# Layer 3's transposed transition matrix: VectorE block transposes into a packed tile in place of TensorE transposes

## The chip, the core and the metric

The kernel runs on one core of a Trainium2 chip. The metric is the device time in microseconds (us) of one execution, the median of several. A core has five engines that run side by side and wait for one another through semaphores: TensorE (matmuls, results in PSUM), VectorE, ScalarE and GpSimd (elementwise work), and SyncE, which here issues the DMAs. In the profile they are PE (with PEld for the loading of weights), DVE, ACT, POOL and SP.

## The reference, cut to what matters

Four graph layers run over 128 graphs of 64 nodes with 512 features. Each layer adds its result to x after a layer norm and a ReLU of its input. Layer 3, the one that is changed, makes a 64x64 transition matrix T for each graph and spreads the features with T and with T squared:

```python
h = jnp.maximum(_layernorm(x, axis=-1), 0.0)
...
Xw = X @ Wv + bv                       # X is h
sj, si = Xw @ aw[:d, 0], Xw @ aw[d:, 0]
e = jax.nn.leaky_relu(sj[:, None, :] + si[:, :, None] + ab[0], negative_slope=0.2)
alpha_matrix = A * jnp.exp(e)
transition = alpha_matrix / (jnp.sum(alpha_matrix, axis=-1, keepdims=True) + 1e-12)
for k in range(Wk.shape[0]):           # 3 steps
    H = H + Xk @ Wk[k] + bk[k]
    Xk = jnp.einsum('bij,bjd->bid', transition, Xk)
return jax.nn.relu(H)
```

So layer 3 is h·W0 + T·h·W1 + T·T·h·W2 plus biases. The adjacency is (128, 64, 64), all numbers are 32-bit floats.

## The kernel before, in words

**Tiling.** A tile is 128 rows of x, that is two graphs; a group is four tiles (T = 4), eight graphs, and there are 16 groups. Each 64x64 matrix of a pair of graphs stands in a 128x128 block-diagonal tile `bd`, [128, 4, 128] for a group. `HALVES` are the two halves of the 128 partitions. Phase 1 runs layers 0 and 1 over all groups and writes the half-finished x to DRAM; phase 2 loads it again and runs layers 2 and 3. The large weight products use a Strassen scheme with seven products (`seven`, `strassen`): every `L595` in the profile is one of its matmuls in layers 0, 1 and 3, and every `L818` one in layer 2.

**What sets the order.** Nothing is issued in the order of the text. Each layer function only records operations (`pe`, `dve`, `act`, `pool`, `dma`) with an estimated cost, the buffers they read and write, and a priority. `Graph.run` then plans: it goes through time, on each engine takes from the operations that can start earliest the one with the smallest priority, gives buffers their slots, and writes the instructions out in that order. The hardware engines execute their queues strictly in that order. A priority is a due time: a base per group (`PERIOD1` or `PERIOD2` times the group's number), plus the progress inside a layer (`step`, scaled by `STRETCH`), plus the offset of the named part in `AT`. All these constants are tuning knobs: they change no result, only the order of the instructions. The planner also overlaps neighbouring groups, so layer 2 of one group stands between the products of layer 3 of the group before.

**Around the change.** In `layer3`, `z` becomes the 64x64 weights of the attention; L904 to L906 sum and invert them by row, and the two L908 write the normalised T into the block-diagonal `tr`. Then TensorE transposes the four 128x128 blocks against the identity (L915) into a PSUM bank, ScalarE copies that bank into plane 0 of the tile `tt` (L917), TensorE multiplies T with it for the transposed square (L921), and ScalarE copies that into plane 1 (L923). The left products `lm` (L936) then multiply h, for each half of the partitions, with both planes: 64 rows of h against `tt.t[half, t, :, half]`, which is 2 x 64 columns, and two copies (L940) bring the result into the layer's Strassen operand `a3`. Only the diagonal 64x64 blocks of `tt` are used there; the tile holds 128 columns per plane, half of them zero. The additions L587 form the Strassen combinations; L565, L567, L953 and L954 take the products out of PSUM, with GpSimd's L949 in between.

Four other lines are named later. L651, L655, L901 and L902 make z, and L651 first waits for a row that two DMAs (L633, L637) have sent through DRAM. L844 are layer 2's 64-column attention scores, L834 and L830 make their query operand, and L879 are layer 2's products with the values, which wait for L854 (the attention weights) and L869 (the values).

**Memory.** PSUM has eight banks (`ps`), shared by all. The list `TWO` places buffers of phase 2 over those of phase 1; `tt` had one slot of [128, 4, 2, 128].

Of the kernel before, what the change touches and what calls it, by code (L numbers as in the profile page):

```python
# [14 lines left out]
P = 128  # L15
C = 64
D = 512
DH = 1024
T = 4
KD = D // P  # L20
KH = DH // P
EPS = 1e-5
HALVES = (slice(0, C), slice(C, P))
# [138 lines left out]
def tile_adj_preln_d4(  # L162
# [6 lines left out]
    nc = tc.nc  # L169
# [18 lines left out]
        ([("tmp", [P, D], 4), ("mB", [P, T, C + 1], 1)], [("s3", [P, 3, 6, P], 1)]),  # L188
        ([("z", [P, DH], 2)], [("hT", [P, KD, T * P], 1)]),
        ([("rT", [P, KH, P], 3)], [("a3", [P, 3 * KD, P], 2)]),  # L190
        ([("s2", [P, 3, 4, P], 1), ("s1", [P, 3, 2, P], 2)], [("vu", [P, 2, D + 1], 2), ("tt", [P, T, 2, P], 1)]),
        ([("y", [P, D], 2)], [("qT", [P, 2, 2 * P], 2)]),
        ([("mT", [P, KD, P], 3)], [("a3", [P, 3 * KD, P], 1)]),
        ([("row", [P, D], 5)], [("sh", [P, 4, 2, 2 * P], 1), ("q", [P, D], 1)]),
# [5 lines left out]
    def size(shape):  # L200
        n = 1
        for d in shape[1:]:
            n *= d
        return n

    for two in TWO:
        both = work.tile([P, max(sum(size(shape) * n for _, shape, n in tags) for tags in two)], F32,
                         name="_".join(tag for tags in two for tag, _, _ in tags))
        for tags in two:
            at = 0  # L210
            for tag, shape, n in tags:
                for i in range(n):
                    v = both[:, at:at + size(shape)]
                    at += size(shape)
                    if len(shape) == 3:
                        v = v.rearrange("p (a b) -> p a b", a=shape[1])
                    elif len(shape) == 4:
                        v = v.rearrange("p (a b c) -> p a b c", a=shape[1], b=shape[2])
# [25 lines left out]
    def c_mm(n, count):  # L244
        return 2 * count * max(n * 2 / 2400 + 0.0025, 0.111)

    TR = 0.109
# [4 lines left out]
    def pe(cost, fn, r, w):  # L252
        return G.op("PE", cost, fn, r, w)

    def dve(cost, fn, r, w):
        return G.op("DVE", cost, fn, r, w)

    def act(cost, fn, r, w):
        return G.op("ACT", cost, fn, r, w)
# [7 lines left out]
    def quad(b):  # L267
        return b.t.rearrange("p (c k) -> p c k", c=4)

    STRETCH, PERIOD1, PERIOD2 = (2.01, 1.52, 3.8, 3.15), 99.32, 100.99
    AT = {
        "x0": -1000.31, "apart": -0.04, "w1": -1140.59, "b1": -730.1, "w2": -692.69, "w": 166.49, "c1": -856.63,
        "l0": -580.98, "c2": -741.75, "l1": 111.32, "c": 219.34, "g0": -1134.91, "g1": -1116.26, "g2": -755.63,
        "g3": -850.44, "g": -1126.24, "l3": 28.03, "wg": 119.55, "w3": 191.39, "last": -98.19, "load1": -120.84,
        "load2": -92.69, "m": -52.0, "h0": -37.33, "p0": -2.35, "z0": -2.26, "q0": 25.57, "y0": -29.58, "h1": -39.25,
        "p1": -17.85, "z1": 10.94, "q1": 12.3, "y1": 27.38, "s": -11.54, "t0": 62.66, "e0": -103.04, "t1": 54.99,
        "e1": -32.68, "hT": -26.23, "sh": 50.82, "lq": 16.73, "pt": 40.17, "v": -3.1, "pv": -184.92, "s3": 16.54,
        "tt": 62.29, "a0": 61.26, "b0": -39.87, "a1": 81.07, "b1_": 65.71,  # L280
    }

    def part(name):
        G.shift = AT[name]


    ident = const.tile([P, P], F32, name="ident")
# [82 lines left out]
    def dot(in0, in1, acc, r, w):  # L370
        j = Buf("o")
        dve(0.77, lambda: nc.vector.scalar_tensor_tensor(j.t, in0(), 1.0, in1(), op0=ALU.mult, op1=ALU.mult,
                                                         accum_out=acc()), r, [*w, j])
# [140 lines left out]
    def pre_stats(g, t):  # L514

        xx, nm = xt[g, t], Buf("nm")
        mv, rs = norm_stats(lambda i: xx.t, 1, [xx])
        pool(0.3, lambda: nc.gpsimd.tensor_scalar(nm.t, mv.t[:, 0:1], rs.t, -1.0, op0=ALU.mult, op1=ALU.mult), [mv, rs], [nm])  # L518
        return nm, rs

    def pre_ln(g, t, stats=None):

        xx, h = xt[g, t], Buf("h")
        nm, rs = stats or pre_stats(g, t)
        act(0.82, lambda: nc.scalar.activation(h.t, xx.t, AF.Relu, bias=nm.t, scale=rs.t), [xx, nm, rs], [h])  # L525
        return h
# [362 lines left out]
    def layer3(g):  # L889

        ad = adjs[g]
        a3, ss = [Buf("a3") for _ in range(T)], [Buf("col"), Buf("col")]
        part("s3")
        stats = [pre_stats(g, t) for t in range(T)]
        for t in range(T):
            h = pre_ln(g, t, stats[t])
            for s in range(2):
                dot(lambda h=h: h.t, lambda s=s: c3_b[:, s, :], lambda t=t, s=s: ss[s].t[:, t:t + 1], [h, ("c3", s)], [(ss[s], t)])
        z = bcast_sum(lambda: ss[1].t, lambda: ss[0].t, [(ss[s], t) for t in range(T) for s in range(2)], extra=kap)
        lrelu(z, 0.2)  # L900
        act(0.42, lambda: nc.scalar.activation(z.t, z.t, AF.Exp), [z], [z])  # L901
        dve(0.42, lambda: nc.vector.tensor_mul(z.t, z.t, ad.t[:, 0]), [z, ad], [z])  # L902
        dn, rn, tr, tt = Buf("col"), Buf("col"), Buf("bd"), Buf("tt")
        dve(0.42, lambda: nc.vector.tensor_reduce(dn.t, z.t, AX.X, ALU.add), [z], [dn])  # L904
        dve(0.16, lambda: nc.vector.tensor_scalar_add(dn.t, dn.t, 1e-12), [dn], [dn])
        dve(0.18, lambda: nc.vector.reciprocal(rn.t, dn.t), [dn], [rn])  # L906
        for s in HALVES:
            dve(0.42, lambda s=s: nc.vector.tensor_mul(tr.t[s, :, s], z.t[s], rn.t[s, :, None].to_broadcast([C, T, C])), [z, rn], [(tr, s.start)])  # L908
        trk, pt, p2 = [(tr, 0), (tr, C)], Buf("ps"), Buf("ps")

        part("tt")

        def mt():
            for t in range(T):
                nc.tensor.transpose(quad(pt)[:, t, :], tr.t[:, t, :], ident)  # L915
        pe(KD * TR, mt, trk, [pt])
        act(0.59, lambda: nc.scalar.copy(tt.t[:, :, 0, :], quad(pt)), [pt], [(tt, 0)])  # L917

        def m2():
            for t in range(T):  # L920
                nc.tensor.matmul(quad(p2)[:, t, :], tr.t[:, t, :], tt.t[:, t, 0, :], start=True, stop=True)  # L921
        pe(c_mm(128, T), m2, [*trk, (tt, 0)], [p2])
        act(0.59, lambda: nc.scalar.copy(tt.t[:, :, 1, :], quad(p2)), [p2], [(tt, 1)])  # L923
        step(2.0)
        for t0 in (0, 2):
            part("a0" if t0 == 0 else "a1")
            for t in (t0, t0 + 1):
                h, b, back = pre_ln(g, t, stats[t]), a3[t], Buf("q")
                transposed(lambda h=h: h.t, [h], Buf("o"), lambda back=back: back.t, [back], lambda b=b: b.t[:, :KD, :], [(b, 0)])

                pq = [Buf("ps"), Buf("ps")]

                def lm(h=h, pq=pq, t=t):
                    for c in range(KD):
                        for i, half in enumerate(HALVES):
                            nc.tensor.matmul(quad(pq[i])[:, c, :], h.t[half, c * P:(c + 1) * P], tt.t[half, t, :, half],  # L936
                                             start=True, stop=True)
                pe(c_mm(128, KD) + 0.2, lm, [h, (tt, 0), (tt, 1)], pq)
                for i, half in enumerate(HALVES):
                    act(0.59, lambda pq=pq, b=b, i=i, half=half: nc.scalar.copy(  # L940
                        b.t[:, KD:, half].rearrange("p (j c) k -> p c j k", j=2),
                        pq[i].t.rearrange("p (c j k) -> p c j k", c=KD, j=2)), [pq[i]], [(b, 1 + i)])
                step(1.0)

            def emit_o(i, j, p, u, v, t0=t0):
                xx, cols, (U, iv) = xt[g, t0 + i], slice(j * D // 2, (j + 1) * D // 2), v
                add, ka = (lambda: bk3_b[:, cols]), "bk3"
                if u is not None:
                    pool(0.88, lambda: nc.gpsimd.tensor_add(U.t[:, iv], U.t[:, u[1]], add()), [u, ka], [v])  # L949
                    add2, ka = (lambda: U.t[:, iv]), v  # L950
                else:
                    add2 = add
                dve(c_v(D // 2), lambda: nc.vector.tensor_add(U.t[:, iv], p.t[:, :D // 2], add2()), [p, ka], [v])  # L953
                dve(c_v(D // 2), lambda: nc.vector.scalar_tensor_tensor(xx.t[:, cols], U.t[:, iv], 0.0, xx.t[:, cols], op0=ALU.max, op1=ALU.add), [v, xx], [(xx, j)])  # L954
                if (i, j) in ((1, 0), (0, 1)):
                    r = (g * T + t0 + i) * P
                    dma(256, lambda: nc.sync.dma_start(out[r:r + P, :], xx.t), [(xx, 0), (xx, 1)], [])

            ak = {}
            for i in range(2):  # L960
                b = a3[t0 + i]
                ak[i, 0] = [(b, 0), (b, 1), (b, 2)]
                ak[i, 1] = [(b, 1), (b, 2)]
            part("b0" if t0 == 0 else "b1_")
            strassen(lambda i, j, t0=t0: a3[t0 + i].t[:, 6 * j:6 * j + 6, :], ak, W3, 6, D // 2, "s3", emit_o)

    def step(us):

        G.prio += us * stretch[0]
# [32 lines left out]
    for k in range(3):  # L1002
        src = Wk3[k].rearrange("(c p) o -> p c o", p=P)
        for c in (0, 2):
            i = k * KD + c
# [69 lines left out]
```

## Time and profile before

| What | Value |
|---|---|
| median of 3 runs | 2401.43 us (2398.42 to 2402.01) |
| profiled execution | 2396.96 us, span 2395.1 us, TensorE clock 0.998 |
| span of phase 1 and phase 2 | about 0 to 1190 and 1190 to 2395 us |
| one group of phase 2 in the steady part | 73.2 us (L915 at 1540.97, the same step of others a multiple of 73.2 later) |
| L915, 64 records | mean 275 ns, 9.8 us busy in all |
| L921, 128 records | mean 276 ns, 17.0 us busy in all |
| L936, 1024 records | mean 278 ns, 65.8 us busy in all |
| L917 and L923, 16 each | 585 ns each |
| L908, 32 | 420 ns each |

A 32-bit matmul shows as two records, a transpose as one. Records of matmuls overlap, because they are pipelined: a mean of 275 ns does not mean that the engine was held for 275 ns, and what a piece of work costs is read from where the next one starts. An entry of the timeline gives start, length, engine, line, tiles, shape and count; brackets at its end hold the idle time just before it and what ended it.

### The profile page before, as it was taken

The page shows a single profiled execution, that of the slowest core. Times are in us where ns is not written, and L with a number is a line of the kernel's source. Part 1 is how long each engine was busy: PE and PEld are TensorE (multiplying, and loading weights), DVE is VectorE, ACT ScalarE, POOL GpSimd, SP SyncE. Part 2 cuts the span into 40 slices and gives each one's busy share as a digit, 9 for nine tenths or more (in the row PEclk, how much of TensorE's full clock was granted, in tenths as well). Part 3 has the DMA queues.
Part 4 walks back from the last instruction along what each step waited for, and adds up shares of the span by engine and source line. Part 5 has one row for each costly group of instructions (what it writes and reads, how often), then busy time and mean ns, then how long its engine had stood idle before and what let it go on. Part 6 is the DMA issues. An engine that isn't in the chain of part 4 may idle for free.

```text
span 2395.1 us, 33543 instructions
## 1 busy us (share of the span) xinstructions
PE 2356.3 (98%) x11930; PEld 1855.0 (77%) x11930; DVE 1721.2 (72%) x3676; ACT 1263.5 (53%) x1754; POOL 938.2 (39%) x1450
## 2 busy tenths in 40 slices
PE   7999999999999999999999999999999999999999
PEld 3576677776777776777778888888888888888887
DVE  7887878787878787877878556666666666666664
ACT  2666565566565566565745445544445444454431
POOL 5234455434455434455344333333333333333321
PEclk9999999999999999999999999999999999999999
DMA  7232222232223222222532232222322222222211
GB/s 242 54 80 47 65 68 71 68 78 51 65 66 73 67 80 52 61 67 77 146 89 62 66 74 55 69 56 58 78 64 60 66 50 71 73 56 64 52 42 36
DMA packets 335928, 168.78 MB, mean 70 GB/s; under 512 B 284688, under 2 KB 290832, under 8 KB 335760
## 3 DMA queue, kind: packets, MB, share of 16 engines
q1 hardware_dynamic: 335760, 166.63, 28.0%
q8 instruction: 94, 1.54, 0.3%
q14 instruction: 74, 0.61, 0.1%
HBM read 64.76 MB, written 34.70 MB: 42 GB/s over the span
## 4 chain that ended last, share of the span: by engine, by line
PE 84%; DVE 6%; DMA 4%; ACT 2%; POOL 2%; issue 2%; SPq 0%; DVEq 0%; POOLq 0%; ACTq 0%
PE ps L595 60%; PE ps L818 11%; PE ps L534 4%; PE ps L936 2%; PE ps L731 2%; PE ps L879 2%; DVE s_s_vu_tt L869 1%; DMA x<-xm 1%; PE ps L844 1%; ACT o L543 1%; DVE bd L854 1%; ACT h L525 1%; POOL u L867 1%; POOL rs L511 1%; DVE st L508 1%
## 5 line engine op out<-in xcount | busy, mean ns | idle before, releaser
L525 ACT ACTIVATE h<-x,nm,rs 128x512 f32<-128x512 f32 x384 | 307.1, 813 | 456.5 <-POOL nm L518 455.3
L595 PE MATMUL ps<-wb_mem,rT_a 128*128 128x256 f32 x2056 | 476.8, 380 | 1.7 <-DVE z_hT L615 0.9
L595 PEld LDWEIGHTS ps<-wb_mem,rT_a 128*128 128x128 f32 x2056 | 386.5, 190 | 74.8 <-issue 20.3
L510 POOL TENSOR_SCALAR rs<-mv 128x1 f32<-128x1 f32 x320 | 101.5, 317 | 534.2 <-DVE mv L509 452.9
L595 PE MATMUL ps<-wb_mem,s_s_vu_tt 128*128 128x256 f32 x1152 | 275.0, 379 | 0.2 <-DVE s_s_vu_tt L587 0.2
L595 PE MATMUL ps<-wb_mem,tmp_mB_s 128*128 128x256 f32 x1152 | 261.3, 379 | 0.2 <-DVE tmp_mB_s L587 0.2
L595 PEld LDWEIGHTS ps<-wb_mem,s_s_vu_tt 128*128 128x128 f32 x1152 | 218.5, 190 | 43.1 <-issue 10.5
L595 PE MATMUL ps<-wb_mem,mT_a 128*128 128x256 f32 x1016 | 240.7, 380 | 1.8 <-ACT u L563 1.3
L595 PEld LDWEIGHTS ps<-wb_mem,tmp_mB_s 128*128 128x128 f32 x1152 | 217.6, 190 | 29.6 <-DVE tmp_mB_s L587 0.6
L595 PE MATMUL ps<-wa_mem,mT_a 128*128 128x512 f32 x512 | 238.0, 593 | 2.1 <-DVE u L567 2.1
L949 POOL TENSOR_TENSOR u<-u,bk_b 128x256 f32<-128x256 f32 x96 | 76.2, 799 | 352.3 <-DVE u L567 292.6
L511 POOL TENSOR_TENSOR rs<-rs,mhalf 128x1 f32<-128x1 f32 x320 | 202.9, 634 | 26.6
L595 PEld LDWEIGHTS ps<-wb_mem,mT_a 128*128 128x128 f32 x1016 | 190.6, 190 | 28.6 <-ACT u L563 1.5
L508 DVE BATCH_NORM_STATS2 st<-x 128x6 f32<-128x512 f32 x256 | 174.1, 680 | 32.4 <-DMA x<-xm 30.8
L595 PE MATMUL ps<-wa_mem,s_s_vu_tt 128*128 128x512 f32 x384 | 182.9, 599 | 1.0 <-ACT c_b L453 0.6
L595 PEld LDWEIGHTS ps<-wa_mem,mT_a 128*128 128x128 f32 x512 | 96.0, 190 | 105.4 <-issue 92.5
L565 DVE TENSOR_TENSOR u<-ps,u 128x256 f32<-128x256 f32 (+1 forms) x160 | 84.4, 527 | 112.1 <-PE ps L595 84.6
L623 POOL TENSOR_TENSOR u<-u,row_sh_q 128x256 f32<-128x256 f32 x96 | 70.9, 746 | 235.0 <-DVE u L565 205.9
L545 ACT COPY rT_a<-z_hT 128x1024 uint16<-128x1024 uint16 x128 | 144.3, 1161 | 4.4 <-DMA z_hT<-tmp_mB_s 4.2
L534 PEld LDWEIGHTS ps<-bd,h 128*128 128x128 f32 x1024 | 129.0, 192 | 16.1 <-issue 8.6
L707 ACT ACTIVATE z_hT<-z_hT 128x512 f32<-128x512 f32 x128 | 79.8, 625 | 116.7 <-DVE z_hT L615 116.6
L563 ACT COPY u<-ps 128x256 f32<-128x256 f32 (+1 forms) x160 | 72.5, 453 | 129.7 <-PE ps L818 71.5
(172 smaller groups left out, 4317.1 us busy)
## 6 DMA issues: line engine op xcount, KB each, us to landing
x<-in_x_dram SPq DMA_DIRECT2D x64, 256.0 KB, 2.8
xm<-x SPq DMA_DIRECT2D x64, 256.0 KB, 2.0
x<-xm SPq DMA_DIRECT2D x64, 256.0 KB, 2.7
out_dram<-x SPq DMA_DIRECT2D x64, 256.0 KB, 2.2
adj<-in_adj_dram SPq DMA_DIRECT2D x32, 256.0 KB, 4.1
rw<-row SPq DMA_DIRECT2D x96, 64.0 KB, 2.8
wb_mem<-in_Wk_dram SPq DMA_DIRECT2D x6, 512.0 KB, 4.4
wa_mem<-in_W1T_dram SPq DMA_DIRECT2D x2, 1024.0 KB, 5.9
```

The lines of the kernel that those rows point to most:

```text
L508: dve(0.69, lambda i=i: nc.vector.bn_stats(st.t[:, i, :], src(i)), [r[i]], [(st, i)])
L510: pool(0.3, lambda: nc.gpsimd.tensor_scalar_add(rs.t, mv.t[:, 1:2], EPS), [mv], [rs])
L511: pool(0.65, lambda: nc.gpsimd.tensor_tensor(rs.t, rs.t, mhalf, ALU.pow), [rs], [rs])
L525: act(0.82, lambda: nc.scalar.activation(h.t, xx.t, AF.Relu, bias=nm.t, scale=rs.t), [xx, nm, rs], [h])
L534: nc.tensor.matmul(quad(p)[:, c, :], h.t[:, c * P:(c + 1) * P], rhs(), start=True, stop=True)
L545: act(1.16, lambda: nc.scalar.copy(u16(dst()).rearrange("p c (k q) -> p c k q", q=2), u16(back()).rearrange("p (q c r) -> p c r q", q=2, c ...
L563: act(n / 1200 + 0.17, lambda: nc.scalar.copy(at(0)(), p1.t[:, :n]), [p1], [(U, 0)])
L565: dve(c_v(n), lambda: nc.vector.tensor_add(at(1)(), p2.t[:, :n], at(0)()), [p2, (U, 0)], [(U, 1)])
L595: nc.tensor.matmul(p.t[:, :n], lhs()[:, c, :], rhs(c), start=first and c == 0, stop=c == kc - 1, skip_group_check=True)
L707: act(0.63, lambda: nc.scalar.activation(z.t[:, cols], z.t[:, cols], AF.Relu), [(z, j)], [(z, j)])
L818: nc.tensor.matmul(pair(p.t)[:, o, :], a, b, start=first and o == 0 and c == 0, stop=c == 1, skip_group_check=True)
L949: pool(0.88, lambda: nc.gpsimd.tensor_add(U.t[:, iv], U.t[:, u[1]], add()), [u, ka], [v])
```

## The change

VectorE can transpose 32x32 blocks from SBUF to SBUF. A 64x64 block is four such blocks, swapped across the diagonal. The change makes the transposed T that way, directly behind L908: for each half of the partitions four instructions, each of which takes a 32 x (4 tiles x 32) block of `tr` to its mirrored place in `tt`. It is for taking the four transposes off TensorE, and with them one PSUM bank, one ScalarE copy and one hand-over between engines. Since the two diagonal blocks of a tile stand on different partitions, `tt` need only hold 64 columns a plane: it is packed to [128, 4, 2, 64], and gets two slots in the memory of the one before. The square then has 64 moving columns for 128, and its copy half the elements. The left products read the same numbers, now from adjacent columns. And the constants of the planner (`STRETCH`, the periods, `AT`) are tuned anew, which reorders the work of all engines in both phases.

```diff
-        ([...], [("vu", [P, 2, D + 1], 2), ("tt", [P, T, 2, P], 1)]),
+        ([...], [("vu", [P, 2, D + 1], 2), ("tt", [P, T, 2, C], 2)]),
...
-    STRETCH, PERIOD1, PERIOD2 = (2.01, 1.52, 3.8, 3.15), 99.32, 100.99
+    STRETCH, PERIOD1, PERIOD2 = (2.01, 0.85, 5.07, 2.81), 97.12, 109.98
     AT = {
-        ... "s3": 16.54, "tt": 62.29, "a0": 61.26, "b0": -39.87, "a1": 81.07, "b1_": 65.71,
+        ... "s3": -5.11, "tt": -20.18, "a0": 57.03, "b0": -53.42, "a1": 66.82, "b1_": 64.98,
...
-        trk, pt, p2 = [(tr, 0), (tr, C)], Buf("ps"), Buf("ps")
+        trk, p2 = [(tr, 0), (tr, C)], Buf("ps")
+
+        B = C // 2
+
+        def blocks(s):
+            for i in range(2):
+                for j in range(2):
+                    nc.vector.transpose(tt.t[s.start + j * B:s.start + (j + 1) * B, :, 0, i * B:(i + 1) * B],
+                                        tr.t[s.start + i * B:s.start + (i + 1) * B, :, s.start + j * B:s.start + (j + 1) * B])
+        for i, s in enumerate(HALVES):
+            dve(1.2, lambda s=s: blocks(s), [(tr, s.start)], [(tt, 2 + i)])

         part("tt")
-
-        def mt():
-            for t in range(T):
-                nc.tensor.transpose(quad(pt)[:, t, :], tr.t[:, t, :], ident)
-        pe(KD * TR, mt, trk, [pt])
-        act(0.59, lambda: nc.scalar.copy(tt.t[:, :, 0, :], quad(pt)), [pt], [(tt, 0)])

         def m2():
             for t in range(T):
-                nc.tensor.matmul(quad(p2)[:, t, :], tr.t[:, t, :], tt.t[:, t, 0, :], start=True, stop=True)
-        pe(c_mm(128, T), m2, [*trk, (tt, 0)], [p2])
-        act(0.59, lambda: nc.scalar.copy(tt.t[:, :, 1, :], quad(p2)), [p2], [(tt, 1)])
+                nc.tensor.matmul(p2.t[:, t * C:(t + 1) * C], tr.t[:, t, :], tt.t[:, t, 0, :], start=True, stop=True)
+        pe(c_mm(64, T), m2, [*trk, (tt, 2), (tt, 3)], [p2])
+        act(0.38, lambda: nc.scalar.copy(tt.t[:, :, 1, :], p2.t[:, :T * C].rearrange("p (t c) -> p t c", t=T)), [p2], [(tt, 1)])
...
-                            nc.tensor.matmul(quad(pq[i])[:, c, :], h.t[half, c * P:(c + 1) * P], tt.t[half, t, :, half],
+                            nc.tensor.matmul(quad(pq[i])[:, c, :], h.t[half, c * P:(c + 1) * P], tt.t[half, t, :, :],
                                              start=True, stop=True)
-                pe(c_mm(128, KD) + 0.2, lm, [h, (tt, 0), (tt, 1)], pq)
+                pe(c_mm(128, KD) + 0.2, lm, [h, (tt, 1), (tt, 2), (tt, 3)], pq)
```

## The prediction

> **What bounds the kernel now.** I read the page's busy shares first, then the 40 slices, then the waits of TensorE, and last the timeline of one middle group.
>
> ```profile
> PE 2356.3 (98%) x11930; PEld 1855.0 (77%) x11930; DVE 1721.2 (72%) x3676; ACT 1263.5 (53%) x1754; POOL 938.2 (39%) x1450
> ...
> PE   7999999999999999999999999999999999999999
> ...
> DVE  7887878787878787877878556666666666666664
> ```
>
> TensorE (PE) is busy in every slice after the first, and layers 2 and 3 run from about slice 20 on, where VectorE (DVE) has a third of its time free. PE is idle for only 2395.1 - 2356.3 = 38.8 us. By stretches of 75 us: 14.7 in the first, 1.9 in the second, 10.1 from 1125 to 1275 (the change of phase), 7.5 in the last 145, and about 0.31 per group in between. That 0.31 is one wait of the value product (L879) each time and has nothing to do with the change. So in the steady groups a TensorE microsecond saved is a microsecond of the span, and a new TensorE wait is paid in full. One steady group, TensorE timeline (start, length, line, tile, count; a matmul's record runs past the start of the next, so I price by differences of starts):
>
> ```profile
> 1527.08 1.16 PE L936 MATMUL ps<-s_s_vu_tt,h 64*128 64x128 f32 x16
> 1528.17 0.69 PE L844 MATMUL ps<-y_qT,z_hT 128*64 128x64 f32 x16
> 1528.78 1.99 PE L818 MATMUL ps<-wa_mem,z_hT 128*128 128x256 f32 x8
> ...
> 1538.38 2.75 PE L595 MATMUL ps<-wb_mem,tmp_mB_s 128*128 128x256 f32 x12
> 1540.97 0.60 PE L915 MATMUL ps<-ident,bd 128*128 128x128 f32 x4
> 1541.41 2.76 PE L595 MATMUL ps<-wb_mem,mT_a 128*128 128x256 f32 x12
> 1544.00 1.05 PE L921 MATMUL ps<-s_s_vu_tt,bd 128*128 128x128 f32 x8
> 1544.89 2.76 PE L595 MATMUL ps<-wb_mem,tmp_mB_s 128*128 128x256 f32 x12
> 1547.58 2.95 PE L936 MATMUL ps<-s_s_vu_tt,h 64*128 64x128 f32 x48
> ```
>
> There is no bracketed idle time: TensorE runs through the transposes (L915) and the square (L921) without waiting. VectorE in the same group:
>
> ```profile
> 1535.49 0.61 DVE L651 TENSOR_TENSOR ee<-rw,col 128x256 f32<-128x256 f32 x1 [0.95 <-DMA rw<-row]
> ...
> 1538.60 0.85 DVE L908 TENSOR_TENSOR bd<-ee,col 64x256 f32<-64x256 f32 x2
> 1539.48 0.42 DVE L567 TENSOR_TENSOR u<-ps,u 128x256 f32<-128x256 f32 x1
> 1539.82 0.41 DVE L954 SCALAR_TENSOR_TENSOR x<-u,x 128x256 f32<-128x256 f32 x1
> 1541.25 0.42 DVE L953 TENSOR_TENSOR u<-ps,u 128x256 f32<-128x256 f32 x1 [1.01 <-PE ps L595]
> ```
>
> T is ready at 1539.45, 1.5 us ahead of L915; behind it VectorE soon idles on TensorE.
>
> **What the Trainium skill says.** "VectorE: DVE Perf Modes", The three transpose paths: VectorE transposes in 32x32 blocks only, into SBUF, and 128x128 bf16 take it 311 ns; TensorE's transpose ends in PSUM. The trace of before has no VectorE transpose; it does show the PSUM copy that TensorE's needs (L917, 585 ns). Same page, Two Vector instructions with no wait between them: an instruction whose input or output starts in another group of 32 partitions than the one before starts only when all earlier ones have finished. The trace agrees: the two L908, on different halves, take 0.85 us for twice 0.42, while L567 to L954 follows after 0.34. So eight block transposes hardly overlap. "TensorE: Matmul & The Clock Gate", LDWEIGHTS (loading the stationary operand): a weight load costs by its columns. The stationary T keeps 128 columns, so halving the moving operand should save little, and L679 (65 moving columns, 0.83 us for 8 records, 629.21 to 630.04) against L921 (128 columns, 0.89) says the same.
>
> **The change, part by part.** There are 16 groups.
>
> 1. TensorE transposes go: 1540.97 to 1541.41 is 0.44 us, with undisturbed neighbours (2.59 us before and after). 16 x 0.44 = 7.0 us saved.
> 2. The square at 64 columns: 0.83 for 0.89, and the product after it loses 0.06 (1.78 for 1.72 after L679) where it lost 0.10 (2.69 for 2.59 after L921). 16 x 0.10 = 1.6 us saved.
> 3. The retuned due times move TensorE's order. In the built order of both programs I counted runs of the small matmuls, which cost a start each. Layer 3's left products: 8 pairs take 1.09 us and 24 take 2.88, so 0.112 a pair and 0.2 a run; layer 2's 64-column scores: 8 take 0.61 and 16 take 1.08 (1207.64 to 1208.72), so 0.14 a run; and a large product beside such a run takes 0.10 longer on that side (1528.78 to 1530.62 is 1.84 for 1.73). Left-product runs rise from 32 to 45 (+2.6 us), score runs fall from 62 to 50 (-1.7), borders rise from 160 to 184 (+2.4): 3.3 us lost.
> 4. ScalarE loses L917 (585 ns) and about half of L923, some 12 us in all; it is half idle, so nothing.
> 5. Eight VectorE transposes of 32 x (4 x 32) per group. From the trace: two-input adds take 0.42 at 256 elements and 0.69 at 512, so 0.285 at 128; the page's price is 0.311 at 128 elements of bf16. Upper bound, should 4-byte elements take two passes: 0.57 (estimate from the first). I take 0.30, 2.4 us a group and 38 us in all, hidden as work. They matter as a wait. Behind them stand L567, needed by the fourth product of layer 3, and through it GpSimd's additions; they run 0.42 later, while the square alone takes 0.9, so the square's wait comes first.
> 6. That wait. Time from the last value products (1520.08 in before, call it 0). New TensorE order up to the square: two value products 0.86, left products 1.19 with their border, product of layer 2 1.93, left products 1.09, layer 3's first product 2.79, scores 0.61, product 1.83, four products of layer 3 10.36, one of layer 2 1.73: 22.4. VectorE: L565 now stands ahead of L651 and needs the third of these layer-3 products, at 15.5 + 0.28 latency; L651 at 16.15 (15.41 in before, where a DMA held it; that DMA is now issued ahead of a transposing DMA, so it should not). L651 to the end of L908 took 3.96 and has as many instructions: 20.1. Plus 8 x 0.30 and 0.06 latency: 22.55. So the square waits about 0.1: 0.03 at 0.285, 0.25 at 0.311, 2.3 at 0.57. Over the twelve groups of this order: 1.2 us lost (0.4 to 28).
> 7. Change of phase: at 1264.06 the first transposes waited 1.88 us for L908, and the scores behind them for L834, queued after L908. From the end of the product before (1262.02) to the end of the scores (1266.68) TensorE needed 1.6 us of 4.66. In the new order three large products and the scores stand between, and two L834 precede L651. I count 2.5 of these 3.06 us as saved.
> 8. The first 50 TensorE steps are the same in both, so the 16 us lost at the start stay; the tail has the same kinds of steps. Two slots for the transposed tile instead of one, in the same memory: no wait on the old one shows in before, so nothing.
>
> Sum: -7.0 - 1.6 + 3.3 + 1.2 - 2.5 = -6.6; 2401.4 - 6.6 = 2394.8.
>
> **The rivals.** A, the wait takes the place of the transposes: at 0.36 a transpose the square waits 0.6, 12 x 0.6 = 7.2, the gain is gone: 2401. For it: no slack is left in step 6, and my VectorE hand-overs are good to 0.3 us. Against: VectorE idles in that stretch, so small delays have somewhere to go. B, slower: 4-byte transposes at the upper bound, 2401.4 - 7.8 + 28 = 2422; or half of that with a collision: two-input VectorE work beside GpSimd stretches (L854, the same form as L908, has a median of 1.33 us against 0.42, with GpSimd's L867 beside it). Against: GpSimd stands still while L908 runs (it waits 13.16 us for L567). C, more gain: the wait is nil, the runs cost nothing, all 3.1 us of step 7 come in, and of the 0.31 wait per group (14 times) 1.3 us go: 2401.4 - 7.0 - 1.6 - 3.1 - 1.3 = 2388. Against: the value products stand in the same pattern behind the same L854 and L869.
>
> **How the numbers follow.** Forecast 0.50, A 0.18, B 0.14, C 0.18. The forecast's band is 2391 to 2397, C's 2386 to 2391, A's 2397 to 2405. The range 2387 to 2403 leaves out B, with an end of A and of C. Faster by over 0.2% (under 2396.6): C and nearly all of the forecast, 0.66; within 0.2%: A and the rest, 0.20; slower: B, 0.14.
>
> **What would show it.** Right: no L915 row; VectorE's eight transposes near 0.30 us each; the 128x64 square near 0.83 us per group with idle before it of 0 to 0.3; the steady period (73.2 us from one L915 to the next) down by about 0.2 (0.54 saved, some 0.25 for the runs, 0.1 waited); the wait at 1264 gone. Wrong: a TensorE wait on the transposes above 0.5 us in every group (A or B), a period shorter by 0.5 or more (C), or a difference in the first 1130 us, where nothing but order moves.

## The result: slower by 0.36%, and the profile after

The changed kernel took 2409.26 us (median of 4 runs, 2405.88 to 2411.21) against 2400.38 for the kernel before on the same chip: a ratio of 1.0036, 95% interval 1.0018 to 1.0053. So it is 8.9 us slower where 6.6 us less were forecast, and outside the predicted range. Line numbers are 4 higher from the square on: L921 is now L925, L923 L927, L936 L940, L940 L944, L949 L953, L953 and L954 L957 and L958. L916 are the VectorE transposes.

The page of the changed kernel, busy shares and slices:

```profile
PE 2359.3 (98%) x11866; PEld 1851.7 (77%) x11866; DVE 1771.8 (74%) x3804; ACT 1249.0 (52%) x1738; POOL 926.1 (39%) x1450
...
PE   8999999999999999999999999999999999999999
...
DVE  7887888787888787877877666676667676666764
```

The 64 TensorE transposes are gone from the count, and VectorE has 50.6 us more to do, 38.7 of it the transposes (128 of 0.302); the other 12 us are not accounted for here. Yet TensorE is no less busy, and its idle time rose from 38.8 to 2404.1 - 2359.3 = 44.8 us. A steady group, timeline of all engines (start, length, engine, line, tiles, count, idle before):

```profile
1534.95 0.42 DVE L565 TENSOR_TENSOR u<-ps,u 128x256 f32<-128x256 f32 x1 [2.33 <-PE ps L595]
1535.29 0.61 DVE L651 TENSOR_TENSOR ee<-rw,col 128x256 f32<-128x256 f32 x1
...
1537.27 2.75 PE L595 MATMUL ps<-wb_mem,tmp_mB_s 128*128 128x256 f32 x12
...
1538.40 0.87 DVE L908 TENSOR_TENSOR bd<-ee,col 64x256 f32<-64x256 f32 x2
...
1539.30 2.52 DVE L916 STREAM_TRANSPOSE s_s_vu_tt<-bd 32x128 f32<-32x128 f32 x8
...
1539.86 1.89 PE L818 MATMUL ps<-wa_mem,z_hT 128*128 128x256 f32 x8
1541.85 0.42 DVE L567 TENSOR_TENSOR u<-ps,u 128x256 f32<-128x256 f32 x1
1541.87 0.97 PEld L925 LDWEIGHTS ps<-s_s_vu_tt,bd 128*128 128x128 f32 x8 [0.52 <-DVE s_s_vu_tt L916]
1541.87 1.10 PE L925 MATMUL ps<-s_s_vu_tt,bd 128*128 128x64 f32 x8
...
1542.81 2.81 PE L595 MATMUL ps<-wb_mem,rT_a 128*128 128x256 f32 x12
```

The square's matmul line has no bracket, but its weight load has: 0.52 us idle, ended by L916. By differences of starts: the product before holds TensorE for 1.73 us, so the square could start at 1541.59 and starts at 1541.87, 0.28 late, the moment the last transpose ends. That is the good case, a clean group from here on; the interval between two clean squares is 73.38 us. In all twelve groups from the third to the fourteenth the square starts 0.05 us after the last transpose. In four of them the wait is 0.5 to 1.1 us, as here (the same view, two lines of one group):

```profile
1684.61 0.62 DVE L651 TENSOR_TENSOR ee<-rw,col 128x256 f32<-128x256 f32 x1 [0.89 <-DMA rw<-row]
...
1691.19 1.10 PE L925 MATMUL ps<-s_s_vu_tt,bd 128*128 128x64 f32 x8 [1.10 <-DVE s_s_vu_tt L916]
```

The row that L651 needs came 0.89 us late, and everything behind it on VectorE with it. The same (0.63 us late) happened in a second of the four; in the third the product that L565 adds was 0.35 us late, and in the fourth ScalarE's exponential L901 was held behind other copies in its queue. TensorE's waits of the changed kernel in sum (total, times, longest), three of its lines, and then the longest one in the timeline:

```profile
PE ps L595 <- ACT u L563: 7.3, 4, 5.3
PE ps L925 <- DVE s_s_vu_tt L916: 6.2, 6, 2.5
...
PE ps L844 <- ACT y_qT L830: 2.8, 1, 2.8
```
```profile
2340.32 4.78 PE L595 MATMUL ps<-wb_mem,mT_a 128*128 128x256 f32 x12 [5.34 <-ACT u L563]
```

L563 is ScalarE's copy of a layer 3 product out of PSUM; on the same engine L525 makes the layer norm's result, L543 packs it for a transposing DMA (L544) and L545 copies what that DMA brings.

The starts of the square say where the time went. The squares do not mark the same amount of other work done in the two kernels, so only long stretches count:

| square of | before | after | after - before |
|---|---|---|---|
| third group | 1397.43 | 1394.40 | -3.0 |
| fourteenth group | 2202.76 | 2206.66 | +3.9 |
| last group | 2346.00 | 2355.68 | +9.7 |
| end of span | 2395.1 | 2404.1 | +9.0 |

Phase 1 is the same (the last group's L679 starts at 1059.81 and 1060.35). The steady stretch loses 6.9 us in 11 intervals (812.26 for 805.33), and the last two groups lose 5.8.

### The profile page after: what moved, and what is told of

It reads as the page before. It is cut to its first block, busy times and chain, and to the rows that moved or that the text cites. A ratio compares the mean times of both kernels' runs of the same rounds, so it can differ in the third digit from the quotient of the medians.

```text
span 2404.1 us, 33462 instructions
## 1 busy us (share of the span) xinstructions
PE 2359.3 (98%) x11866; PEld 1851.7 (77%) x11866; DVE 1771.8 (74%) x3804; ACT 1249.0 (52%) x1738; POOL 926.1 (39%) x1450
## 4 chain that ended last, share of the span: by engine, by line
PE 81%; DVE 8%; DMA 4%; ACT 3%; issue 2%; POOL 2%; SPq 0%; DVEq 0%; POOLq 0%; ACTq 0%
PE ps L595 55%; PE ps L818 12%; PE ps L534 4%; PE ps L731 2%; PE ps L940 2%; PE ps L879 2%; DVE s_s_vu_tt L916 1%; PE ps L844 1%; DMA x<-xm 1%; DVE bd L854 1%; ACT h L525 1%; DVE s_s_vu_tt L869 1%; DMA out_dram<-x 1%; PE ps L925 1%; PE ps L469 1%
## 5 line engine op out<-in xcount | busy, mean ns | idle before, releaser
L525 ACT ACTIVATE h<-x,nm,rs 128x512 f32<-128x512 f32 x384 | 308.3, 813 | 462.2 <-POOL nm L518 460.3
L595 PE MATMUL ps<-wb_mem,rT_a 128*128 128x256 f32 x2080 | 482.3, 380 | 2.8 <-ACT u L563 1.9
L595 PEld LDWEIGHTS ps<-wb_mem,rT_a 128*128 128x128 f32 x2080 | 391.4, 190 | 75.3 <-issue 19.8
L953 POOL TENSOR_TENSOR u<-u,bk_b 128x256 f32<-128x256 f32 x96 | 77.3, 811 | 370.4 <-DVE x L958 190.4
L565 DVE TENSOR_TENSOR u<-ps,u 128x256 f32<-128x256 f32 (+1 forms) x160 | 84.1, 526 | 133.1 <-PE ps L595 71.1
L623 POOL TENSOR_TENSOR u<-u,row_sh_q 128x256 f32<-128x256 f32 x96 | 76.6, 806 | 237.8 <-DVE u L565 212.2
L545 ACT COPY rT_a<-z_hT 128x1024 uint16<-128x1024 uint16 x128 | 144.6, 1162 | 5.8 <-DMA z_hT<-tmp_mB_s 5.5
L563 ACT COPY u<-ps 128x256 f32<-128x256 f32 (+1 forms) x160 | 72.7, 454 | 124.5 <-PE ps L818 82.6
L543 ACT COPY tmp_mB_s<-z_hT 128x1024 uint16<-128x1024 uint16 x128 | 133.8, 1045 | 6.3 <-DVE bk_b L500 1.7
```

The costliest lines, as they stand in the source:

```text
L543: act(1.05, lambda: nc.scalar.copy(u16(planes.t).rearrange("p (q c) -> p q c", q=2), u16(src()).rearrange("p (c q) -> p q c", q=2)), ksrc, ...
L545: act(1.16, lambda: nc.scalar.copy(u16(dst()).rearrange("p c (k q) -> p c k q", q=2), u16(back()).rearrange("p (q c r) -> p c r q", q=2, c ...
L565: dve(c_v(n), lambda: nc.vector.tensor_add(at(1)(), p2.t[:, :n], at(0)()), [p2, (U, 0)], [(U, 1)])
L595: nc.tensor.matmul(p.t[:, :n], lhs()[:, c, :], rhs(c), start=first and c == 0, stop=c == kc - 1, skip_group_check=True)
L623: pool(0.75, lambda: nc.gpsimd.tensor_add(U.t[:, iv], U.t[:, iu], row()[:, cols]), [u, krow], [v])
```

## The experiments

Theory: the square's wait behind VectorE's chain costs the steady stretch, and a copy stuck in ScalarE's queue costs the tail. Rival at first: the tuned constants, not the transposes, cost the time.

| run | median us | ratio to before, 95% interval |
|---|---|---|
| e1_old_times | 2420.47 | 1.0082, 1.0068 to 1.0097 |
| e2_new_times | 2436.96 | 1.0146, 1.0132 to 1.0160 |
| e3_half | 2398.76 | 0.9993, 0.9985 to 1.0002 |
| e4_twice | 2473.76 | 1.0304, 1.0290 to 1.0318 |
| e5_square_later | 2441.50 | 1.0175, 1.0161 to 1.0189 |
| e6_last_group | 2411.62 | 1.0047, 1.0034 to 1.0060 |
| e7_both | 2441.12 | 1.0172, 1.0158 to 1.0186 |
| e8_tensor_transposes_twice | 2406.79 | 1.0032, 1.0019 to 1.0044 |
| e9_chain_earlier | 2403.45 | 1.0016, 1.0008 to 1.0023 |
| e10_chain_and_tail | 2401.23 | 1.0005, 0.9996 to 1.0014 |
| e12_first_group | 2404.32 | 1.0023, 1.0013 to 1.0034 |
| e13_row_transfer_only | 2411.99 | 1.0053, 1.0040 to 1.0065 |
| e14_without_transfer | 2407.66 | 1.0038, 1.0026 to 1.0049 |
| e15_exponential_first | 2408.16 | 1.0039, 1.0026 to 1.0052 |

**Constants against code.** e1 is the changed code with the constants of before, e2 the code of before with the new ones:

```diff
 # e1 (e2 is the reverse edit on the kernel before)
-    STRETCH, PERIOD1, PERIOD2 = (2.01, 0.85, 5.07, 2.81), 97.12, 109.98
+    STRETCH, PERIOD1, PERIOD2 = (2.01, 1.52, 3.8, 3.15), 99.32, 100.99
     ... (and all of AT)
```

> The changed code with the planner's constants of before (STRETCH, periods, AT). Theory A (the retuned order loses the time, not the VectorE transposes): the transposes and the narrow square are worth 8.6 us of TensorE, the small-matmul runs stay near before (34 and 61 runs for 32 and 62), and the square comes about 0.8 us after the transposes are ready, so 2391 to 2396. Theory B (the transposes' own wait or their delay of VectorE's queue loses it): a wait of the square on the transposes in every group, 2403 to 2412.

> The kernel before with the retuned constants alone. Theory A: slower than before, 2404 to 2416, with TensorE waits on ScalarE's L563 as in the changed kernel. Theory B: as before, 2396 to 2403.

Both are much slower than either kernel: 2420.47 and 2436.96. e1 has new waits of 4.0 us at the change of phase and of 5.2 us in the tail; e2 one of 12.3 us at the TensorE transposes. Each set of constants fits its own code, so the loss as a whole can't be split into a part of the code and a part of the constants, and neither theory's numbers held. But e1's trace settles one thing. With the old constants, too, the square starts 0.05 us after the last transpose in all twelve steady groups (1852.47 after 1852.41 in one), and from the third to the fourteenth square e1 takes 811.12 us, the changed kernel 812.26, the kernel before 805.33. So the wait in the steady groups is not the work of the new constants.

**The work of the transposes.** e3 makes four of the eight block transposes per group and leaves out the other half of T transposed, e4 makes each one twice, in unchanged order:

```diff
 # e3
-                for j in range(2):
+                for j in range(1):
 # e4
-            for i in range(2):
+            for i in (0, 0, 1, 1):
```

> The changed kernel with only four of the eight block transposes (it leaves out half of T transposed), the order of all other instructions unchanged. If the square waits on the transposes as the trace says, its wait of about 0.28 us in the steady groups and the longer ones (0.83, 0.46, 1.10, 1.05 us, 2.52 at the change of phase) go or shrink by 1.26: 2400 to 2404. If these waits only stand in for others: 2407 to 2410.

> The changed kernel with each block transposed twice, other order unchanged. The square then waits 2.5 us more in each of 16 groups: 2409 + 40 = 2449 if nothing gives way, under 2420 if VectorE's slack takes it.

1.26 us less VectorE work per group brought the clean interval from 73.38 to 73.0 us and the whole time down by 10.5 us; the stretch from the third to the fourteenth square took 805.58 us for 812.26. VectorE was not the busiest engine: the value lies in where those microseconds stand. The tail's wait stayed (5.35 us). The opposite sign, e4, shows a second price. The same kind of wait, and the layer 3 product behind the square, in two groups of e4 (timeline of TensorE):

```profile
1487.49 1.10 PE L925 MATMUL ps<-s_s_vu_tt,bd 128*128 128x64 f32 x8 [3.52 <-DVE s_s_vu_tt L916]
1488.43 4.50 PE L595 MATMUL ps<-wb_mem,mT_a 128*128 128x256 f32 x12
...
1565.24 1.10 PE L925 MATMUL ps<-s_s_vu_tt,bd 128*128 128x64 f32 x8 [2.80 <-DVE s_s_vu_tt L916]
1566.19 2.81 PE L595 MATMUL ps<-wb_mem,rT_a 128*128 128x256 f32 x12
```

After the wait of 3.52 us the product took 4.50 instead of 2.81, and the granted clock from 1489 to 1491 was 0.51. Eleven of e4's products behind the square took 4.2 to 4.5 us in this way, so e4 lost 48.5 us in waits and 1.4 to 1.7 us more in each of these.

**The price of what was removed.** e8 is the kernel before with the TensorE transposes issued twice:

```diff
-            for t in range(T):
+            for t in [*range(T), *range(T)]:
                 nc.tensor.transpose(quad(pt)[:, t, :], tr.t[:, t, :], ident)
```

> The kernel before with each of layer 3's TensorE transposes of T issued twice into the same PSUM tile (four more per group; the result is unchanged): the price of what the change removed. Theory 1 (0.44 us a group, TensorE being the bound): 16 x 0.44 = 7.0 us, to 2407-2408 us. Rival a (the second set fills part of the gap in which the square waits for the copy, or is otherwise hidden): 2401-2404 us. Rival b (the later copy makes the square wait, as it has little slack): 2411 us or more.

Measured: 7.0 us more (2406.79 against 2399.80 for the kernel before, run beside it), and intervals of 73.63 us for 73.20. Four transposes cost 0.43 us a group in full.

**Moving the square.** e5 changes the order on two engines, e6 one constant, e7 does both:

```diff
 # e5, TensorE in 12 groups (V: a layer 2 product, S: a layer 3 product)
-V (L818)   square (L925)   S (L595)
+S (L595)   square (L925)   V (L818)
 # e5, VectorE
-L916 L567 L869 L957 L958 L957 L958
+L916 L567 L957 L958 L957 L958 L869
 # e6
-"last": -93.01
+"last": -98.19
```

> The changed kernel, where in the steady groups the square changes places in a way that gives VectorE more time: TensorE's order V product (1.73 us), square, S product (2.59 us) becomes S product, square, V product, so the square stands 0.86 us later; on VectorE the addition behind the V product (L869) moves behind the four additions L957/L958. No instruction is added or removed. Theory 1 (the loss of the changed kernel's middle is the square's wait on VectorE's transposes, in most groups 0.3 us and up to 1.1 us where the row transfer comes late, some 10 us in all): the waits of up to 0.86 us vanish, the clean interval between squares falls from 73.38 to 73.0-73.1 us, and the time falls by 6 to 10 us, to 2399-2403 us. Rival (the wait only moves: the left products now wait for the later V product's addition to free its PSUM tile, or the transposes for the later rows): waits of about 0.3 us per group appear at L940, and the time stays at 2406-2411 us.

> The changed kernel with one constant of the planner as before: the last group's due time (AT last -93.01 becomes -98.19). It changes the order of the last 85 us alone: the last group's V product and its PV products come earlier, and ScalarE's copy of the first S product is no longer behind four layer norms. Theory 1 (the tail loses 5.3 us in one wait for that copy, and 2 us more in the product after it, which took 4.78 instead of 2.75 us): the wait of 5.3 us goes, and the time falls by 5 to 7.5 us, to 2402-2404.5 us. Rival (the last group's chain from its statistics to the square is what bounds the tail, so the wait turns up at the square of the last group instead): a wait of 3 us or more at the last L925, time 2406-2409 us.

> The two edits together: the square later in the steady groups and the last group's due time as before. Theory 1 (the two losses are separate and account for the result): the gains add, to 2391-2396 us, 5 to 9 us below the kernel before. Rival (one of them is only moved, or a cause not named stands behind): 2399 us or more, no better than before.

e5 took 2441.50 us: neither theory saw what it hit. Two lines of its steady group:

```profile
1551.76 0.42 DVE L567 TENSOR_TENSOR u<-ps,u 128x256 f32<-128x256 f32 x1
...
1552.24 2.86 PE L595 MATMUL ps<-wb_mem,rT_a 128*128 128x256 f32 x12 [2.30 <-DVE u L567]
```

The S product writes the PSUM tile that L567 reads, and L567 stands behind the transposes on VectorE. In the twelve groups these waits sum to 30.1 us, and the time rose by 32.2. So the square is only the first of the two that wait for this queue, as step 5 of the prediction had said: with a fourth S product in its place the wait of a clean group is 2.3 us instead of 0.3.

e6 took 2411.62 us, above both ranges. The wait for L563 left, and another came, not at the last square as the rival had it, but at an S product, for the copy of a left product that stands behind the layer norms:

```profile
2345.50 2.08 PE L595 MATMUL ps<-wb_mem,mT_a 128*128 128x256 f32 x4 [5.62 <-ACT mT_a L944]
```

From the fourteenth square to the end e6 takes 198.9 us, the changed kernel 197.4. The rest of the difference lies ahead of the edit, where nothing was changed, so all that e6 says is that nothing was gained. e7 (2441.12) is as slow as e5, has the waits of both, and says nothing of its own.

**Starting the chain earlier.** e9 leaves TensorE's order alone and moves three operations, in 12 or 13 steady groups each:

```diff
 # VectorE
-L565 L651 L655
+L651 L655 L565
 # ScalarE
-L545 L543 L901
+L901 L545 L543
 # SyncE
-L633 L544 L637
+L633 L637 L544
```

> The changed kernel with TensorE's order untouched and the chain that ends in the transposes started earlier, in the steady groups: on VectorE the two operations on the row sum (L651, L655) stand ahead of the addition L565 for which VectorE sat idle 2.3 us; the row's second transfer (L637) stands ahead of the transposing DMA behind which it waited; ScalarE's exponential (L901) stands ahead of a copy that it stood behind. No operation is added, taken away or shortened. Theory 1 (the middle of the changed kernel loses to the square's wait behind VectorE's in-order chain, 0.3 to 1.1 us a group, the same 10 us that half the transposes gave): the transposes end some 2 us earlier, the square's waits go, the clean interval falls from 73.38 to 73.0-73.1 us and the time by 7 to 11 us, to 2398-2402 us. Rival (the transposing DMA that is now later, or VectorE's addition L565, holds other work, as L567 did in the square-later kernel): the interval stays or grows, 2408 us or more.

```profile
1530.64 0.62 DVE L651 TENSOR_TENSOR ee<-rw,col 128x256 f32<-128x256 f32 x1
...
1532.98 0.43 DVE L565 TENSOR_TENSOR u<-ps,u 128x256 f32<-128x256 f32 x1 [1.26 <-PE ps L595]
...
1536.47 2.52 DVE L916 STREAM_TRANSPOSE s_s_vu_tt<-bd 32x128 f32<-32x128 f32 x8
...
1537.89 1.89 PE L818 MATMUL ps<-wa_mem,z_hT 128*128 128x256 f32 x8
...
1539.62 1.00 PE L925 MATMUL ps<-s_s_vu_tt,bd 128*128 128x64 f32 x8
...
1540.46 2.81 PE L595 MATMUL ps<-wb_mem,rT_a 128*128 128x256 f32 x12
```

The transposes now end at 1538.99, before the square's turn; it starts 1.73 us after the product, without a wait. They end 1.10 us after the start of that product, where they ended 1.96 after it: 0.86 us earlier, not the 2 us expected, since the rest of the chain stands behind L565, which still waits for its product. It was enough in all twelve groups. The clean interval is 72.99 us, the 11 intervals are 805.25 us (after 812.26), and the time is 2403.45: 5.8 us down (4.8 by the two ratios), a little short of what was expected. e10 and e12, which contain the same edit, have 805.80 and 806.65 for the 11 intervals. With the same work on every engine and TensorE's order untouched, the loss of the steady stretch is gone.

Three further runs take e9 apart: e13 is its SyncE edit alone, e15 its ScalarE edit alone, e14 the VectorE and ScalarE edits without SyncE's. Their diffs are those parts of e9's.

> The changed kernel with one part of the earlier chain alone: in the steady groups the row's second transfer L637 is issued ahead of the transposing DMA L544 behind which it stood. VectorE's, ScalarE's and TensorE's orders are untouched. Theory 1 (in the groups with a wait of 0.5 to 1.1 us the row's late arrival holds the chain; in the others the addition L565 does): these waits fall to 0.3 us, the clean interval stays at 73.4 us, and the time falls by 2 to 4 us, to 2405-2407.5 us. Rival a (the transfer never held it): 2409 us. Rival b (it is the whole of the loss): 2399-2402 us.

> The earlier chain without its transfer part: VectorE's two row operations L651 and L655 ahead of L565, and ScalarE's exponential L901 ahead of a copy (L545, which waits for a transposing DMA) and a pack (L543); the row's transfer stays where the changed kernel has it. Theory 1 (the in-order queues of VectorE and ScalarE hold the chain, the transfer hardly): nearly all of the earlier chain's gain, clean interval 73.0-73.1 us, 2402.5-2405 us. Rival (the row arrives just as L565 ends, so that without the earlier transfer the first edit moves nothing): clean interval 73.3-73.4 us, 2406-2409 us.

> The changed kernel with one part of the earlier chain alone: in the steady groups ScalarE's exponential L901 stands ahead of the copy L545 and the pack L543. Theory 1 (in the groups with a long wait the exponential is held behind the copy that waits for its transposing DMA; in the others L565 holds the chain): the clean interval stays at 73.4 us, the waits of 0.5 to 1.1 us fall to 0.3-0.9 us, 2406-2408 us. Rival (ScalarE's queue is the whole of it): clean interval 73.0 us, 2402-2405 us. Second rival (it is no part of it): 2409-2412 us.

None of them does it: 2411.99, 2407.66 and 2408.16 us, with clean intervals of 73.38, 73.33 to 73.37 and 73.38, and 812.67, 811.35 and 810.30 us for the 11 intervals. e15 did what the theory had for it, within 0.2 us, and e13 and e14 went to a rival (e13 to rival a). In e13 the row came early and nothing came of it, since the transposing DMA that now ran later held ScalarE (timeline, one group; L545 copies what that DMA brings, L901 is the exponential in the chain):

```profile
1686.93 1.16 ACT L545 COPY rT_a<-row_sh_q 128x1024 uint16<-128x1024 uint16 x1 [1.50 <-DMA row_sh_q<-o]
...
1688.94 0.41 ACT L901 ACTIVATE ee<-ee 128x256 f32<-128x256 f32 x1
...
1694.43 1.10 PE L925 MATMUL ps<-s_s_vu_tt,bd 128*128 128x64 f32 x8 [1.00 <-DVE s_s_vu_tt L916]
```

In e14 VectorE waited 2.19 us for the row instead of for the S product (1534.37, L651). The chain stands in three in-order queues at nearly the same place; freeing one shows the next. Of what was tried only all three together took the wait away. VectorE's edit alone, and SyncE's together with one of the other two, were not run, so it is not shown that all three are needed.

**The tail and the first group.** e10 adds to e9 the tail's edit, e12 to that an edit in layer 3's first group:

```diff
 # e10, ScalarE, last group (and one L587 four operations earlier on VectorE, L901 ahead of one L545)
-L525 L525 L543 L525 L944 L563
+L944 L563 L525 L525 L543 L525
 # e12, first group: TensorE
-square  L844  left products (2 runs)  L818
+L844  L818  square  left products (2 runs)
 # e12, VectorE
-L916 L834
+L834 L916
```

> The kernel with the earlier chain, and in the last group also ScalarE's copy of the first S product (L563) and a copy of a left product (L944) ahead of the layer norms that wait for the statistics, and one addition L587 in a gap of VectorE. Theory 1 (the tail's 5.3 us wait is ScalarE's in-order queue, and the last group's chain is 3 us shorter when it no longer stands behind L565): the wait of 5.3 us becomes two of 1 to 2 us, the last square stands 3 to 4 us earlier, and the time is 2-4 us below the kernel with the earlier chain alone: 2394-2399 us. Rival (the last group's chain alone bounds the tail, and the fill in front of it is used up whatever ScalarE's order is): no more than 1 us below, the wait turning up at the last L925.

> The kernel with the earlier chain and the mended tail, and one more edit in layer 3's first group, where the square waits 2.5 us: on VectorE the addition L834 stands ahead of the transposes instead of behind them, and on TensorE the score run L844 and one Q product L818 (1.73 us) that need it stand ahead of the square. Theory 1 (that wait, too, is VectorE's in-order queue, with 0.9 us to 1.1 us left once there is other work to run): 1.3 us less, and 1 to 3 us more where the clock no longer falls after a wait of 2.5 us: 2397-2400 us, at or just below the kernel before. Rival (left products and their copies now come later and hold the S products): the same 2401 us or more.

e10 is 2401.23 us, 2.2 below e9 but above its range: the 5.3 us wait is three of 0.6, 2.0 and 2.4 now, the last one at the last group's square, where the rival had it; so the last group's chain from its statistics to the square holds the tail next. No difference from the kernel before can be measured (0.9996 to 1.0014), so I have no version that beats it. e12 (2404.32) fell to its rival in time, by another wait than the rival's: it turned up at L818, for an L869 that also stands behind the transposes.

```profile
1274.46 2.85 PE L818 MATMUL ps<-wa_mem,row_sh_q 128*128 128x256 f32 x8 [2.46 <-DVE s_s_vu_tt L869]
```

## Why the prediction was wrong, step by step

1. **TensorE's transposes**, 7.0 us: right, e8 measured 7.0.
2. **The square**, 1.6 us: wrong in size, nothing was saved. It takes 0.84 us (1539.62 to 1540.46 in e9) for 0.89, but the product after it takes 2.74 for 2.69: together 3.58 us, as in the kernel before.
3. **More runs of small matmuls**, 3.3 us lost: not measured by itself. e9's clean period, where the square does not wait, is 0.21 below before's; with the 0.43 of step 1 saved that leaves 0.22 lost a group, 3.5 us by 16. That fits, but it is a remainder, not a measurement of the runs.
4. **ScalarE's copy**, 0: right as far as the copy goes. But ScalarE's order decides two of the waits found here, and "half idle, so nothing" was no reason to leave its queue out of step 6.
5. **The price of a VectorE transpose**, 0.30 us: right, 299 to 308 ns and eight in 2.52. The Trainium skill's 311 ns ("VectorE: DVE Perf Modes", The three transpose paths), stated for bf16, holds here for 4-byte elements of 32 x (4 x 32) as well: they did not take twice as long. Eight of them in a row cost 0.12 us more than the sum's 2.40.
6. **The square's wait**, 1.2 us: the step that failed most, and by the size of the term. The mechanism was the one foreseen, and a clean group came out to about 0.1 us: counted as in the prediction (0 is 1519.20 here), the square's turn was at 22.39 for 22.4, L651 at 16.09 for 16.15, L651 to L908 took 3.98 for 3.96, and the square started at 22.67 for 22.55. But where no slack is left each tenth is paid. The wait was 0.28, and the next product came 0.94 us after the start of a square that had waited, 0.84 after one that had not: 0.38 us in a clean group where the sum had 0.1, 4.2 us in 11 intervals. Another 2.8 us came from the four late groups, where the row's DMA, which "should not" hold L651, did so twice, and the exponential in ScalarE's queue, which was not in the sum, once. Together the steady stretch paid 7.0 us (812.26 against 805.25 in e9). That rival A said 7.2 is luck: it took 0.36 us for a transpose, and they take 0.302.
7. **The change of phase**, 2.5 us saved: the wait of 1.88 us went, and 2.79 (L844 for L830) and 2.52 us (the square for L916) came. Of the 2.52, 0.84 us are not the transposes' own: in this group the two L908 took 1.69 us for 0.85. GpSimd's L867 ran beside the first of them (until 1266.76), the collision that rival B had set aside; that it is the cause is not shown. TensorE's idle time from 1185 to 1320 fell from 8.8 to 8.2 us, 0.6 for 2.5. The squares are 3.0 us ahead at the third group, but with other work left over.
8. **The tail**, 0: the other step that failed. It lost 5.1 us after the fourteenth square. In the new order the last group's statistics start at 2327.46, when S products at 2319.67 and 2326.58 have already started; TensorE then has one more (2332.11) before it waits. In the kernel before they start at 2316.81, and four S products (2318.09 to 2326.72) follow. ScalarE's layer norms wait for the statistics, and L944 and L563 stand behind. The wait of 5.34 us was followed by a product of 4.78 us for 2.75. e10 shows what the order on ScalarE, with one addition on VectorE, is worth, 2.2 us; the rest of this step is read from the trace. "The same kinds of steps" is no argument about order.

Beside the steps, two steady groups wait 0.96 and 0.59 us for L563 behind a layer norm whose x came late; before has no such wait. Summed from the forecast: 5.8 more in step 6, about 5.1 in step 8, 1.9 in step 7, 1.6 in step 2, 0.2 in step 3, 1.5 for these two waits: 16.1, against 15.5 found. Steps 6 and 8 alone turned the sign.

## What to carry to other kernels

Work moved to an engine with idle time isn't free when it is put in the last link of a chain that a full engine waits for; what counts is the slack of that one wait, and everything queued behind the new work waits too (here L567, L834 and L869). Before calling such a wait small, walk every in-order queue that the chain crosses, with the DMA and the neighbours in front of each link, and look at the worst group as well as the clean one. When one queue is freed and nothing happens, free the others before dropping the theory.

## What was unexpected of the hardware

The clock falls after shorter waits than I had counted on, and not every time. In e9 and e10 the first group has the same wait of 2.5 us for L916, in the same order of instructions; the left products behind it (L940, 32 records) then took 1.99 and 3.72 us by starts. The windows 1265 to 1275 and 1275 to 1290 (length, TensorE busy, records, granted clock, DMA share, GB/s), first of e9, then of e10:

```profile
1265.00:1275.00 10.00, 7.48 (x74) 1.00 0.22 53
1275.00:1290.00 15.00, 15.00 (x71) 1.00 0.00 1
```
```profile
1265.00:1275.00 10.00, 7.50 (x52) 0.79 0.22 53
1275.00:1290.00 15.00, 15.00 (x82) 0.91 0.01 2
```

The next square came 44.71 us later in e9 and 47.81 in e10: 3.1 us lost by the clock after one wait of 2.5 us. The loss comes in steps. In the nine runs that have this wait (2.50 to 2.71 us) and this order, the interval is 44.7 us in four (the changed kernel, e6, e9, e14), 46.3 in three (e5, e13, e15) and 47.8 in two (e7, e10), and the granted clock from 1264 to 1280 is 1.00, 0.89 and 0.79.

The Trainium skill ("TensorE: Matmul & The Clock Gate", What's actually happening) has the clock halved after an idle window of about 3.4 us; here waits of 2.5 to 2.7 us were enough in five runs of nine. Of eight waits of 2.80 or 2.81 us in e4, five were followed by a product of 4.5 us and three by one of 2.8; in the kernel before the clock was 0.84 from 1265 to 1275, after its wait of 1.88. So a wait of this length can cost up to about twice its length, and these runs don't show what decides it. It may be one source of scatter, but hardly the only one: e9 ranged from 2397.41 to 2407.37, and the kernel before, run beside it, from 2393.42 to 2404.02. Medians of such kernels need many runs.
